# Five outer sums moved from VectorE to adding transfers, and two more pairs of products split into quarters

## The chip, the cores and the metric

The kernel runs on one core of a Trainium2 chip. The metric is the device time of one execution in microseconds (us). Engines are named as in the profile: PE is TensorE's matmul and PEld its weight load, DVE is VectorE, ACT is ScalarE, POOL is GpSimd, SP is SyncE, which issues most loads.

## What is computed

Eight batches of 256 tokens with 1024 features, in float32. Two layers, each with a residual:

```python
# layer 0, with a mask of its own for every batch b
sign = 2 * mask - 1                                  # (8, 1024, 1024)
x = x + (x @ W0.T + b0) + (x @ sign) * coeff[b]
# layer 1, with an adapter of rank 16 picked for every batch
x = x + (x @ W1.T + b1) + 2.0 * (x @ A[slot]) @ B[slot]
```

## The kernel before, in words

All data is kept transposed (features on the 128 partitions, tokens along the free dimension), so that the result of one layer is the moving operand of the next. The weight of layer 0 is made on the chip for each batch: ScalarE turns a block of the mask into numbers (line 453), VectorE adds the dense weight (line 364, `add`). The residual is an identity added to the weight.

Large products are made by Strassen's scheme in Winograd's form: seven products of half size in the place of eight, with sums of blocks before and after. Each level has four sums for the left factor (s1 to s4), four for the right factor (t1 to t4), and reads that add the products into the output.

- *First layer.* `seven(b)` (line 677) makes one batch by seven products (`product`, matmuls at line 720, 128 columns each). Its sums of weights and tokens are VectorE's. Product X of s3 and t3 is read by `finish(1, 1, "X")` (line 732 to 734), and afterwards TensorE adds the product of a22 and t4 into the same bank X; so that last product waits for this read.
- *Second layer.* After four batches (a group) `second_layer(group, before)` (line 968) multiplies W1 with the group's four results y, seen as one matrix of 2 x 2 blocks. Here Winograd's scheme stands twice: the outer seven products are the runs 0 to 6, in the order A11, A12, S1, S2, S4, S3, A22; a run is made of seven inner products of 256 x 256 x 256, four matmuls of 256 columns each (line 1003). The third run is S1, the fourth S2.

An outer sum of y (`outer_t`, line 978) makes a run's right factor: two instructions of 128x1024 on VectorE. The outer sums of W1 are made once, in the first group: S1, S3 and S2 by `outer_w1_moved` (line 903), a scaled copy on ScalarE (line 912) followed by a transfer from SBUF to SBUF that adds the other operand to it (line 920, issued by GpSimd); S4 on VectorE. The first group also stores all leaves of W1 (line 835, GpSimd's queue), and the second loads them again (`left_again`, line 853).

Some inner products are split a third time. Class `Deep` (line 1014) makes one of 256 x 256 x 256 from seven matmuls of 128 columns (line 1058), which accumulate in a chain: ScalarE copies the first (line 1071), VectorE takes sums out of the chain after the sixth and the seventh (lines 1080 and 1087). Each needs four sums of its left leaf and three instructions for its right factor (lines 1028 to 1037) first. `THIRD` names the runs whose products X (a11) and Z (s1) are made so, `LATE` those where Y (a12) and the last product into X (a22) are. Two methods of `Run` belong to it: `xz`, which issues the pair of quartered products and puts pieces of the run before (`rest`: its z4 and x4, or x3) between them, and `y4`, the same for the late pair, with pieces of x2 between. In a late run the first product is read directly into two outputs, where another run copies bank X to Y on ScalarE.

```python
THIRD = {1: (0, 2, 3, 4, 6)}
LATE = {1: (0, 1)}
BIG, SMALL, BANKS = 34, 16, 8
```

Buffers are 34 big ones (128x1024), 16 small ones (128x512) and the 8 banks of PSUM.

*The order of work.* Nothing is issued in the order of the code. Each instruction is a task of `Plan` with an engine, a duration, the tasks that it needs, and often a due time. TensorE's order is the program's; `order` (line 137) lays out the other engines by a simulation: for each engine the task that can start first, among equals the one with the earliest latest start, `ls`, worked back from when its readers are due. `ahead` bars a task until so long before that. The laid-out order is then fixed; on the chip each engine works through its own list and waits by semaphores. A transfer is taken to need its issue, a latency (2.8 us on POOL's queue) and its bytes at 396e3 per us. A task with `hop` set is one that TensorE waits for soon: VectorE is not given another task that would end over 0.05 us after such a task can start, or after its `ls` where that is later; if nothing shorter is there, VectorE is left idle.

Of the kernel before, what the change touches and what calls it, by code (L numbers as in the profile page):

```python
# [17 lines left out]
DENSE = (0,)  # L18
EARLY = (1,)
SCALING = 2.0  # L20
THIRD = {1: (0, 2, 3, 4, 6)}
LATE = {1: (0, 1)}
BIG, SMALL, BANKS = 34, 16, 8


# [29 lines left out]
class Plan:  # L55
# [10 lines left out]
    MARGIN = 0.3  # L66
    TIGHT = 1.0
    FAR = 3.0
    HOP = 0.05

    def __init__(self, start):
        self.tasks = []
# [3 lines left out]
    def task(self, engine, busy, tail, emit, reads=(), writes=(), due=None, ahead=None, nbytes=0):  # L76
        k = Task()
        k.engine, k.busy, k.tail, k.emit, k.due, k.ahead = engine, busy, tail, emit, due, ahead
        k.n, k.bytes, k.rank, k.hop = len(self.tasks), nbytes, None, False
# [12 lines left out]
        for r in writes:  # L92
            for key in r.keys:
                self.writer[r.buf, key] = k
                self.readers[r.buf, key] = []
        k.bufs = list(dict.fromkeys(r.buf for r in [*writes, *reads]))
        for b in k.bufs:
            b.left += 1
        k.open = len(k.before)
        k.ready = 0.0  # L100
        k.done = False
        if engine == "PE":
            k.due = self.pe
            self.pe += busy
        self.tasks.append(k)
        return k
# [30 lines left out]
    def order(self, slots, idle):  # L137
# [40 lines left out]
            return min(ok)  # L178

        out = []  # L180
        hops = [k for k in self.tasks if k.hop]
        while len(out) < len(self.tasks):
            best = None
            held = None
# [2 lines left out]
            for e in free:  # L187
# [8 lines left out]
                else:  # L196
# [15 lines left out]
                    elif soon and idle[e] and k.ls > s + self.FAR:  # L212
# [73 lines left out]
def kernel(  # L286
# [55 lines left out]
    def small(name, a, b):  # L342
        return Buf(name, "S", (a, b))
# [333 lines left out]
    def seven(b, leave=False):  # L677
# [143 lines left out]
    SOON = 12.0  # L821
    A_OF = {"a11": (0, 0), "a12": (0, 1), "a22": (1, 1)}

    def left_first(name):
        leaves = {n: w1_block(name, *uv) for n, uv in A_OF.items()}
        a = {(u, v): w1_block(name, u, v) for u in range(2) for v in range(2)}
        own = OWN.get(name, INNER)

        def keep(n):
            at = leaf_dram[name, n] = Buf(  # L830
                f"leaf_{name}_{n}",
                None,
                t=dram.tile([P, CG, OQ], F32, tag=f"{name}{n}", name=f"leaf_{name}_{n}"),
            )
            dma("POOL", at((0,)), leaves[n], P * 512 * 4, due=plan.pe + 25.0)

        for n in A_OF:
            if n in own:
                keep(n)
        for n, op, x, z in (  # L840
            ("s1", "add", a[1, 0], a[1, 1]),
            ("s2", "sub", "s1", a[0, 0]),
            ("s3", "sub", a[0, 0], a[1, 0]),
            ("s4", "sub", a[0, 1], "s2"),
        ):
            s = small(f"{name}_{n}", CG, OQ)
# [3 lines left out]
            keep(n)  # L850
        return leaves

    def left_again(name, pairs=()):
# [44 lines left out]
    def outer_w1(name, op, x, z, into=None):  # L898
        q = quads[name] = quads[into] if into else [pair(f"w1_{name}_{u}") for u in range(2)]
        for u in range(2):  # L900
            add(q[u](ALL), quads[x][u](ALL), quads[z][u](ALL), 1024, op)

    def outer_w1_moved(name, sign, x, z, into=None):

        q = quads[name] = quads[into] if into else [pair(f"w1_{name}_{u}") for u in range(2)]
        for u in range(2):
            o, a, b = (r(ALL) for r in (q[u], quads[x][u], quads[z][u]))
            plan.task(
                "ACT",
                1024 / 1200 + 0.06,  # L910
                0.11,
                lambda o=o, a=a: nc.scalar.mul(o.ap(), a.ap(), sign),
                (a,),
                (o,),
            )
            plan.task(
                "POOL",
                0.53,
                2.8,
                lambda o=o, b=b: nc.gpsimd.dma_start(o.ap(), b.ap(), accum_op=ALU.add),  # L920
                (o, b),
                (o,),
                nbytes=3 * P * 1024 * 4,
            )

    def behind(o, late):
        plan.task(
# [35 lines left out]
            )  # L963

    READ = (15.0, 4.0)
    UV = [(0, 0), (0, 1), (1, 1), (1, 0)]

    def second_layer(group, before):
# [45 lines left out]
        class Deep:  # L1014
# [62 lines left out]
            def second(self):  # L1077
                i = self.i
                u = self.chain((0,), lambda t: t[:, 0])
                k = add(self.quarter(0, 1), u, self.fifth.sb((i,), lambda t: t[:, i, 1]), P)  # L1080
                k.hop = True

            def third(self):
                i = self.i
                u = self.chain((0,), lambda t: t[:, :1].to_broadcast([P, 2, P]))
                o = self.ps((0,), lambda t: t[:, 1].rearrange("p (v o) -> p v o", v=2))
                k = add(o, u, self.fifth.sb(("zero", i), lambda t: t[:, i]), 2 * P)
                k.hop = True

        class Fifth:  # L1090

# [96 lines left out]
            return [("a11", "s1")] * (n in deep) + [("a12", "a22")] * (n in late)  # L1188

        def leaves_of(name):  # L1190
            left[name] = left_first(name) if first else left_again(name, pairs(OUTER.index(name)))

        class Run:
            def __init__(self, n, seed, out, dest=None, then=None):
# [383 lines left out]
```

## Time and profile before

| | |
|---|---|
| median of 3 runs | 398.2 us (397.63 to 399.25) |
| profiled execution, own time | 397.7 us |
| its span, first to last instruction | 396.0 us |
| clock granted to TensorE | 1.00 |
| PE busy | 392.3 us (99%), 2836 records |
| PEld busy | 363.2 us (92%) |
| DVE busy | 350.2 us (88%), 516 instructions |
| ACT busy | 154.2 us (39%), 281 instructions |
| POOL busy | 52.7 us (13%), 101 instructions |
| HBM, read and written | 64.25 and 19.92 MB |

One matmul in float32 shows as two records. In the span the dense first batch goes up to 34.8 us, the first layer of the first group to 109.8, its second layer to 202.5, the second group's first layer to 299 and its second layer to the end. Rows of the profile name the line of `kernel.py` that issued an instruction; most of VectorE's are line 364, so the shapes tell them apart. Durations of one instruction on VectorE are a little longer than the distance to the next, because neighbours overlap.

### The profile page before, as it was taken

How to read it: one execution, taken by the hardware profiler on the slowest of the kernel's cores; microseconds unless marked ns; L12 is line 12 of the kernel's file. 1: busy time of each engine (PE TensorE's matmuls, PEld its weight loads, DVE VectorE, ACT ScalarE, POOL GpSimd, SP SyncE). 2: the span in 40 equal slices, each digit the busy share in tenths (PEclk: the TensorE clock that was granted, in tenths of full speed). 3: DMA queues.
4: the chain of work that ended last, by engine and by line, in shares of the span. 5: the costliest groups of instructions: out<-in, count | busy, mean ns of one | idle time of the engine just before them, and what ended most of it. 6: DMA issues, size and time to landing. Idle time of an engine off the chain costs nothing.

```text
span 396.0 us, 7306 instructions
## 1 busy us (share of the span) xinstructions
PE 392.3 (99%) x2836; PEld 363.2 (92%) x2836; DVE 350.2 (88%) x516; ACT 154.2 (39%) x281; POOL 52.7 (13%) x101
## 2 busy tenths in 40 slices
PE   9999999999999999999999999999999999999997
PEld 7889999999978888888899999999999789998896
DVE  3559999999997789997999999999976989899876
ACT  5784675612534121008417276372222322210210
POOL 1000000131653353140134000000000000000000
PEclk9999999999999999999999999999999999999999
DMA  8999999460699889878479655111000357753844
GB/s 285 391 389 410 407 408 365 149 226 26 183 263 282 281 278 370 339 270 318 165 283 323 214 211 223 69 55 55 0 28 18 119 161 236 227 148 118 273 134 168
DMA packets 32724, 87.79 MB, mean 222 GB/s; under 512 B 4530, under 2 KB 5170, under 8 KB 32690
## 3 DMA queue, kind: packets, MB, share of 16 engines
q1 hardware_dynamic: 26064, 67.19, 47.5%
q0 software_dynamic: 6336, 19.94, 15.8%
q8 instruction: 22, 0.36, 0.4%
q10 hardware_dynamic: 290, 0.20, 0.2%
q14 instruction: 12, 0.10, 0.1%
HBM read 64.25 MB, written 19.92 MB: 213 GB/s over the span
## 4 chain that ended last, share of the span: by engine, by line
PE 99%; DVE 0%; issue 0%
PE bank L720 44%; PE bank L1003 37%; PE bank L534 7%; PE bank L1058 6%; PE bank L1162 2%; PE bank L1131 2%; PE bank L399 1%; PE bank L1352 0%; PE bank L412 0%; DVE big L364 0%
## 5 line engine op out<-in xcount | busy, mean ns | idle before, releaser
L364 DVE TENSOR_TENSOR big<-big,big 128x1024 f32<-128x1024 f32 (+2 forms) x112 | 115.0, 1044 | 3.2 <-PE bank L720 2.1
L720 PE MATMUL bank<-small,big 128*128 128x128 f32 x896 | 104.0, 275 | 0.0
L720 PEld LDWEIGHTS bank<-small,big 128*128 128x128 f32 x896 | 102.0, 192 | 0.0
L364 DVE TENSOR_TENSOR big<-bank,big 128x512 f32<-128x512 f32 (+2 forms) x107 | 70.6, 676 | 18.2 <-PE bank L1003 11.8
L720 PE MATMUL bank<-big,big 128*128 128x128 f32 x672 | 78.3, 275 | 0.0
L1003 PE MATMUL bank<-small,small 128*128 128x256 f32 x328 | 78.2, 380 | 0.0
L720 PEld LDWEIGHTS bank<-big,big 128*128 128x128 f32 x672 | 76.8, 192 | 0.1
L453 ACT ACTIVATE big<-big,neg_c,two_c 128x1024 f32<-128x1024 int32 (+2 forms) x65 | 70.6, 1124 | 9.9 <-DMA big<-mask 9.8
L364 DVE TENSOR_TENSOR big<-big,w 128x1024 f32<-128x1024 f32 (+2 forms) x65 | 67.7, 1073 | 6.0 <-ACT big L453 4.3
L1003 PEld LDWEIGHTS bank<-small,small 128*128 128x128 f32 x328 | 61.2, 190 | 8.6 <-issue 0.8
L631 ACT ACTIVATE big<-bank,b 128x128 f32<-128x128 f32 x112 | 32.0, 369 | 61.8 <-PE bank L720 61.8
L368 ACT COPY bank<-bank 128x512 f32<-128x512 f32 (+1 forms) x32 | 13.7, 430 | 91.7 <-PE bank L1058 35.4
L1003 PE MATMUL bank<-big,small 128*128 128x256 f32 x168 | 41.2, 380 | 0.0
L368 ACT COPY big<-bank 128x512 f32<-128x512 f32 x32 | 17.6, 593 | 53.2 <-PE bank L1162 27.4
L1003 PEld LDWEIGHTS bank<-big,small 128*128 128x128 f32 x168 | 30.8, 190 | 4.3 <-DVE big L364 0.4
L534 PE MATMUL bank<-small,big 128*128 128x256 f32 x128 | 29.3, 393 | 0.0
L534 PEld LDWEIGHTS bank<-small,big 128*128 128x128 f32 x128 | 25.3, 199 | 3.7
L364 DVE TENSOR_TENSOR small<-big,small 128x512 f32<-128x512 f32 (+1 forms) x49 | 27.5, 571 | 0.4
L1003 PE MATMUL bank<-big,big 128*128 128x256 f32 x112 | 26.7, 381 | 0.0
L1003 PEld LDWEIGHTS bank<-big,big 128*128 128x128 f32 x112 | 21.0, 190 | 3.4 <-DVE big L364 0.4
L1097 POOL MEMSET small<- 128x256 f32 x7 | 2.2, 310 | 155.1 <-PE bank L720 78.9
L1058 PE MATMUL bank<-small,big 128*128 128x128 f32 x154 | 22.4, 275 | 0.0
(59 smaller groups left out, 268.7 us busy)
## 6 DMA issues: line engine op xcount, KB each, us to landing
big<-mask SPq DMA_DIRECT2D x56, 512.0 KB, 7.3
big<-xT SPq DMA_DIRECT2D x14, 512.0 KB, 6.7
big<-mask SPq DMA_DIRECT2D x16, 256.0 KB, 5.4
w<-w0T SPq DMA_DIRECT2D x16, 256.0 KB, 5.4
big<-w1T SPq DMA_DIRECT2D x8, 512.0 KB, 5.8
leaf_S_s<-small POOLq DMA_DIRECT2D x16, 256.0 KB, 5.8
outT<-big POOLq DMA_DIRECT2D x16, 256.0 KB, 3.0
outT<-big SPq DMA_DIRECT2D x15, 256.0 KB, 2.3
```

The costliest lines, as they stand in the source:

```text
L364: return dve(lambda: f(o.ap(), x.ap(), y.ap()), n, (x, y), (o,), due, ahead)
L368: "ACT", n / 1200 + 0.06, 0.11, lambda: nc.scalar.copy(o.ap(), x.ap()), (x,), (o,), due
L399: nc.tensor.matmul(idle_ps.t[:, 0, :n], lhsT=zeros[:, :P], rhs=zeros[:, :n], start=True, stop=True)
L453: lambda: nc.scalar.activation(o.ap(), x.ap(), AF.Identity, bias=neg_c.t[:, b : b + 1], scale=two_c.t[:, b : b + 1]),
L534: nc.tensor.matmul(dense[ot // 2].t[:, ot % 2, :], lhsT=w_b0[c].t[:, h, j * P : (j + 1) * P], rhs=x0[c // CG].t[:, c % CG, :], start=c == ...
L631: lambda o=o, p=p, bias=bias: nc.scalar.activation(o.ap(), p.ap(), AF.Identity, bias=bias.ap()),
L720: nc.tensor.matmul(ps[:, j, :], lhsT=l[:, c, j * P : (j + 1) * P], rhs=m[:, 2 * a + c, :], start=first and a == 0 and c == 0 and j == 0, s ...
L1003: nc.tensor.matmul(ps.t[:, j, :], lhsT=lt[:, c, j * P : (j + 1) * P], rhs=rt[:, c, :], start=start and c == 0 and j == 0, stop=False, skip ...
L1058: lambda: nc.tensor.matmul(o.ap(), lhsT=l.ap(), rhs=r.ap(), start=start, stop=False, skip_group_check=True),
L1097: plan.task("POOL", 0.4, 0.1, lambda: nc.gpsimd.memset(z.ap(), 0.0), (), (z,), ahead=5.0)
L1131: nc.tensor.matmul(ph.t[i * S : i * S + R, 0, :], lhsT=la.t[:, i, c, :], rhs=y[GB * group + i, c // TPH].t[:, c % TPH, :], start=c == 0, s ...
L1162: nc.tensor.matmul(ps[b].t[:, j, :], lhsT=lb_pad.t[rows, o : o + P], rhs=h_sb.t[rows, :], start=j == 0, stop=j == 1, skip_group_check=True,)
```

## The change

The outer sums of y for S2 and A22 in the first group and for S2, S3 and A22 in the second are made as the moved sums of W1: a copy on ScalarE that turns the sign, and an adding transfer issued by GpSimd. A22 is now built in the buffers of S2 and no longer in those of a block of y. The first group's third run (S1) gets its products X and Z in quarters, for which `left_first` makes the sums of the leaves; with that, z4 of its second run is no longer issued at that run's end but between the quarters, and so is x4. The second group's fourth run (S2) gets the late pair too. The planner's figures for a moved sum change (0.9 us of issue for 0.53, two times the bytes for three). `hop` becomes a number, and the read of X at row 1, column 1 of each batch of the first layer gets one: -1.0, so that VectorE is kept free from 1 us before that read can start or has to start at the latest, whichever is later.

```diff
-THIRD = {1: (0, 2, 3, 4, 6)}
-LATE = {1: (0, 1)}
+THIRD = {0: (2,), 1: (0, 2, 3, 4, 6)}
+HOP, READ_HOP = 0.05, -1.0
+LATE = {1: (0, 1, 3)}
...
-                    if e == "DVE" and not k.hop and pe_at < len(pe):
+                    if e == "DVE" and k.hop is None and pe_at < len(pe):
                         lag = max(0.0, free["PE"] - pe[pe_at].due)
                         for h in [h for h in hops[:4] if not h.done]:
                             u = self.near(h, lag)
-                            if u is None or s >= u or s + k.busy <= max(u, h.ls) + self.HOP:
+                            if u is None or s >= u or s + k.busy <= max(u, h.ls) + h.hop:
                                 continue
-                            until = max(u, h.ls) + self.HOP
+                            until = max(u, h.ls) + h.hop
...
         def finish(i, v, n):
             o = y[b, i]((v,), lambda t: t[:, :, v * H : (v + 1) * H])
-            add(o, banks[n]((0,)), o, OH, due=plan.pe + 20.0)
+            k = add(o, banks[n]((0,)), o, OH, due=plan.pe + 20.0)
+            if n == "X" and i == 1 and v == 1:
+                k.hop = READ_HOP
...
-    def left_first(name):
+    def left_first(name, pairs=()):
...
+        leaves["deep"] = {}
+        for n in [n for two in pairs for n in two]:
+            l = leaves[n]
+            sums = small(f"ls_{name}_{n}", 4, P)
+            s = leaves["deep"][n] = [sums((i,), lambda t, i=i: t[:, i]) for i in range(4)]
...
+            for o, op, x, z in (
+                (s[0], "add", block(0, 1), block(1, 1)),
+                (s[1], "sub", s[0], block(0, 0)),
+                (s[2], "sub", block(0, 0), block(0, 1)),
+                (s[3], "sub", block(1, 0), s[1]),
+            ):
+                add(o, x, z, P, op, ahead=SOON)
         return leaves
...
+    def moved(o, sign, x, z):
+
+        plan.task(
+            "ACT", 1024 / 1200 + 0.06, 0.11, lambda: nc.scalar.mul(o.ap(), x.ap(), sign), (x,), (o,)
+        )
+        plan.task(
+            "POOL",
+            0.9,
+            2.8,
+            lambda: nc.gpsimd.dma_start(o.ap(), z.ap(), accum_op=ALU.add),
+            (o, z),
+            (o,),
+            nbytes=2 * P * 1024 * 4,
+        )
...
+    MOVED = (("S2", "A22"), ("S2", "S3", "A22"))
...
             for v in range(2):
-                add(whole(right[name][v]), whole(x[v]), whole(z[v]), 1024, "sub")
+                if name in MOVED[group]:
+                    moved(whole(right[name][v]), -1.0, whole(z[v]), whole(x[v]))
+                else:
+                    add(whole(right[name][v]), whole(x[v]), whole(z[v]), 1024, "sub")
...
-            outer_t("A22", b21, right["S2"], into=b21)
+            outer_t("A22", b21, right["S2"], into=right["S2"])
```

More of the change, by code (lines that the diff above doesn't have):

```diff
@@ L68 @@
     FAR = 3.0
-    HOP = 0.05
     def __init__(self, start):
@@ L78, in task @@
         k.engine, k.busy, k.tail, k.emit, k.due, k.ahead = engine, busy, tail, emit, due, ahead
-        k.n, k.bytes, k.rank, k.hop = len(self.tasks), nbytes, None, False
+        k.n, k.bytes, k.rank, k.hop = len(self.tasks), nbytes, None, None
         k.before, k.after = {}, []
@@ L180, in order @@
         out = []
-        hops = [k for k in self.tasks if k.hop]
+        hops = [k for k in self.tasks if k.hop is not None]
         while len(out) < len(self.tasks):
@@ L850, in left_first, with block @@
             keep(n)
+        leaves["deep"] = {}
[3 more added lines that the diff above has]
+            s = leaves["deep"][n] = [sums((i,), lambda t, i=i: t[:, i]) for i in range(4)]
+            def block(c, j):
+                return l.buf(l.keys, lambda t, f=l.index: f(t)[:, c, j * P : (j + 1) * P])
+            for o, op, x, z in (
[5 more added lines that the diff above has]
+                add(o, x, z, P, op, ahead=SOON)
         return leaves
@@ L906, in outer_w1_moved @@
         for u in range(2):
[L907 to L924, printed above, removed]
+            moved(q[u](ALL), sign, quads[x][u](ALL), quads[z][u](ALL))
     def behind(o, late):
@@ L1080, in second @@
                 k = add(self.quarter(0, 1), u, self.fifth.sb((i,), lambda t: t[:, i, 1]), P)
-                k.hop = True
+                k.hop = HOP
             def third(self):
@@ L1087, in third @@
                 k = add(o, u, self.fifth.sb(("zero", i), lambda t: t[:, i]), 2 * P)
-                k.hop = True
+                k.hop = HOP
         class Fifth:
@@ L1190, in leaves_of @@
         def leaves_of(name):
-            left[name] = left_first(name) if first else left_again(name, pairs(OUTER.index(name)))
+            left[name] = left_first(name, pairs(OUTER.index(name))) if first else left_again(name, pairs(OUTER.index(name)))
         class Run:
```

## The prediction

> **What bounds the kernel now.** I read the page first, then the chain of waits in order of time, the table by stage, and last the rows of the instructions that the change adds or removes. The page:
>
> ```profile
> span 396.0 us, 7306 instructions
> PE 392.3 (99%) x2836; PEld 363.2 (92%) x2836; DVE 350.2 (88%) x516; ACT 154.2 (39%) x281; POOL 52.7 (13%) x101
> ...
> PE   9999999999999999999999999999999999999997
> ...
> PE 99%; DVE 0%; issue 0%
> ```
>
> TensorE is busy for 392.3 of 396.0 us, and the chain that ended last is TensorE for 99%. A busy digit alone does not prove a dense stream, since ends are modelled; so the chain in order of time, which goes by starts (start, length, what):
>
> ```profile
> 327.08 2.23 PE bank L1058 x20
> ...
> 358.08 9.07 PE bank L1003 x42
> ...
> 391.41 1.77 PE bank L1352 x12
> 393.18 0.02 issue
> 393.20 0.29 DVE big L364
> ```
>
> A matmul of this program shows as two records. 9.07/42 = 0.216 us per record of 256 columns and 2.23/20 = 0.1115 us per record of 128 columns; every long piece of the chain has these two pitches, so TensorE stands still almost nowhere. What isn't its work is 396.0 - 392.3 = 3.7 us, and nearly all of that is the start (first matmul at 0.9 us) and the end (last one done at 393.2), which the change doesn't touch. So the kernel's time is the count of its matmuls. Other engines only matter where they make TensorE wait. By stage (first layer, second layer, for each of the two groups; columns: length, busy time of PE, PEld, DVE, ACT, POOL, clock, DMA share, GB/s):
>
> ```profile
> 34.80:109.80 75.00, 75.00 (x674) 75.00 (x673) 74.53 (x87) 37.61 (x73) 13.88 (x24) 1.00 0.71 261
> 109.80:202.50 92.70, 92.70 (x523) 79.00 (x522) 80.99 (x114) 27.57 (x42) 30.03 (x53) 1.00 0.86 288
> 202.50:299.00 96.50, 96.50 (x867) 96.50 (x866) 91.79 (x108) 45.19 (x87) 5.91 (x12) 1.00 0.38 135
> 299.00:396.00 97.00, 94.16 (x641) 83.48 (x639) 83.59 (x170) 20.19 (x50) 1.56 (x5) 1.00 0.51 163
> ```
>
> VectorE is nearly full in the first layers, and has 11.7 and 13.4 us free in the second layers, where the change works. The transfers' share is 0.86 in the first group's second layer and 0.51 in the second group's.
>
> One rule of the Trainium skill reads this otherwise: "Perfetto Trace Analysis", section "Identifying the Most-Contended Engine", says that matmul busy time is no measure of the headroom and that weight-load busy time is. By it 396.0 - 363.2 = 32.8 us would be open; the chain's pitches leave 3.7 us, and I go by them.
>
> **TensorE's work (the gain).** A product of 256 x 256 x 256 is four matmuls of 256 columns: 8 records x 0.216 = 1.73 us. As quarters it is seven of 128 columns: 14 x 0.1115 = 1.56 us. That saves 0.167 us each; 0.16 with the pitch of 0.112 that longer runs of 128 columns show (34.81 to 109.85 us, 672 records). Four products change: X and Z of the first group's third run, and Y and the last product into X (the leaves a12 and a22) of the second group's fourth. 4 x 0.16 = 0.64 us, all on the path, because TensorE is the path. Nothing else in the diff removes a matmul. z4 and x4 of the first group's second run move into the gaps between the quarters, z4 and x3 of the second group's fourth into the next run's; their count stays.
>
> **VectorE.** Removed: ten outer sums of 128x1024, four in the first group (S2, A22) and six in the second (S2, S3, A22), at 1.22 us in the rows by form: 4.9 and 7.3 us. Added in the first group: 8 sums of 128 columns for the left quarters (0.28 each: 2.3), per product one of 256 and two of 128 for the right ones (0.42 + 0.57: 2.0 for both), and the two sums that feed TensorE's next quarter, which have rows of their own:
>
> ```profile
> L364 DVE TENSOR_TENSOR bank<-bank,small 128x256 f32<-128x256 f32 x14 | 5.4, 428 | 3.1 <-PE bank L1058 3.1
> L364 DVE TENSOR_TENSOR bank<-bank,small 128x128 f32<-128x128 f32 x14 | 3.5, 293 | 1.4 <-PE bank L1058 1.4
> ```
>
> 0.43 + 0.29, twice: 1.4. Together 5.7 against 4.9 removed: 0.8 us more in a stage with 11.7 us free. In the second group: four left sums of 256 columns (1.7), right ones 2.0, feeding ones 1.4, and two more reads of a bank, since a product is now read into two outputs (2 x 0.69 = 1.4): 6.5 against 7.3, 0.8 us less. So for VectorE the transfers pay for the quarters and neither leaves a gain; it wasn't the path. What hides these sums is the free time of the second layers. Were that cover gone, they would cost what doesn't fit, at most the 5.7 and 6.5 us.
>
> The new reservation (VectorE is kept free from 1 us before the read at line 734 of each batch's lower right product) adds no work but can hold VectorE idle in the first layers. Bounds: a gain is excluded, as no matmul of line 720 waits there now; the loss is up to 1.0 us plus one 1.22 us sum per batch, three batches of the first group where only 0.47 us is free: 3 x 2.2 - 0.5 = 6.1 us. I take 0: the read's turn comes while 16 other matmuls (3.6 us) stand before the product that needs it.
>
> **ScalarE, GpSimd, queues.** Ten scaled copies at 1.06 us (the row of line 912) go to ScalarE, which is busy 27.6 of 92.7 and 20.2 of 97.0 us. In return the fourth run's 0.57 us copy falls away; four copies of a quarter (0.25) and two of a pair (0.37) come. Queued behind a scaled copy are copies out of banks that TensorE reuses, so one may come 1.06 us later; the waits of ScalarE on TensorE (35.4 us on line 1058) say that it is early as a rule. GpSimd issues ten transfers:
>
> ```profile
> L920 POOL DMA_DIRECT2D big<-big x6: 876/900/1231, 104.8 to 131.5; - x6
> ...
> DMA to landing us min/median/max: 4.8/7.2/11.0
> ```
>
> That is 9 us of issue. GpSimd waits in order for the scaled copy before each, and behind it in the first group stand stores of leaves and of output, whose late landing holds buffers; in the second only the small memsets for the quarters (0.31 us). A moved sum now takes 1.06 + 0.9 + 7.2, some 9 us, where VectorE took 1.22. The trace says that there is time: VectorE does pairs of 128x1024 sums at 113.64 and 117.12 us, and the third run's inner sums for the next factor start only past 139 us.
>
> ```profile
> 113.64 2.35 DVE L364 TENSOR_TENSOR big<-big,big 128x1024 f32<-128x1024 f32 x2
> ...
> 139.19 1.28 DVE L364 TENSOR_TENSOR small<-big,small 128x512 f32<-128x512 f32 x2
> ```
>
> Even 11.0 us fits into 25. The second group has the same length of run and half-free transfers. So cost 0, with an upper bound below. The skill's "DMA: Bandwidth & Descriptors", section on the anatomy of a DMA on the gpsimd path, gives 2.0 us plus bytes/436e3, an estimate of 3.2 us for 512 KB; these rows show 7.2, and the rows decide.
>
> **New waits.** Quarters have a chain of their own: TensorE, ScalarE's copy, VectorE's sum, TensorE. The fourteen quartered products now in the trace (196 records of line 1058) lose almost nothing: the worst piece is 12 records in 1.47 us where 12 x 0.1115 = 1.34, 0.13 us in all. For two pairs more I take 0 and keep 0.3 us as the upper end.
>
> **Sum.** The profiled execution took 397.7 us, its span 396.0, so 1.7 lie around it. 397.7 - 0.64 = 397.06. The median of the runs is 398.2, 0.5 above the profiled one; on that footing the sum is 397.56, and I predict **397.6 us**.
>
> **Rivals.** (1) *The new quarters stall a little.* Each of four products has two feeding sums; at 0.08 us each, half of the shortest wait of VectorE on a quarter in its timeline (0.16 us), 8 x 0.08 = 0.64 us eats the gain: 398.2. For it: VectorE is busy 15.70 of the 16.6 us from 131.4 to 148, where the first group's pair falls, and its first quarter comes a product (1.73 us) sooner than the third run starts now. Against it: 196 records of quarters with 0.13 us lost.
>
> (2) *A moved sum lands late and holds VectorE, slower.* Place: the first group, where transfers are busiest (shares of 1.05 and 1.02 from 109.8 to 131.4 us and 1.00 from 148 to 164). VectorE's order is fixed beforehand with a landing of 0.9 + 2.8 + 1.05 MB / 396e3 = 6.35 us; if it is 11.0, the first inner sum stands at the head of VectorE's queue for up to 4.6 us, and behind it the reads and the feeding sums that TensorE waits for. TensorE never makes that up: 398.2 - 0.64 + 4.6 = 402.2, or about 400.4 for a wait of 2.8. It decides from where the wait outlasts what TensorE has in hand by 2.6 us. For it: 11.0 us stands in the rows, and six transfers of the same kind share the queue then. Against: the 25 us above.
>
> (3) *Faster by more than 2 us*: needs stalls to remove, and the 3.7 us are start and end. Only chance between runs is left.
>
> That the quarters or transfers aren't made as described can't be excluded but has no sign in the diff.
>
> **How the numbers follow.** Forecast 0.53, rival 1 0.15: both within 0.5% (2.0 us, about what a measurement of this kernel can tell from no change). Rival 2 0.20, and other waits of that size (the reservation's, late buffers) 0.07: slower, 0.27. Rival 3 0.05: faster. The runs of before spread from 397.63 to 399.25, -0.6 and +1.0 about their median; 397.6 with that and 0.3 of stall makes 397.0 to 398.9 for the forecast alone. The range must reach into rival 2: 396.7 to 401.2.
>
> **What would show it.** Right: line 1058 (or its new number) with 56 more records, the product line with 32 fewer, PE busy near 391.7, still no PE wait behind VectorE, and the last matmul done near 392.5. VectorE's busy time within 1 us of 350.2, ScalarE's up by 11. Wrong: pieces of the chain with a pitch above 0.112 or 0.216 us, or with VectorE or a transfer in them; where they lie (after 136 us, after 340 us, or in the first layers) would tell rivals 1, 2 and the reservation apart.

## The result, and the profile after

The changed kernel takes 401.12 us (399.97 to 401.95, six runs) against 397.76 us of the kernel before in the same runs: a ratio of 1.0076, interval 1.0054 to 1.0099. It is slower, where no change was forecast; it lies inside the stated range (396.7 to 401.2) because that range was stretched to reach into rival 2. The page of the profiled execution (401.16 us):

```profile
span 399.5 us, 7452 instructions
PE 392.9 (98%) x2860; PEld 363.6 (91%) x2860; DVE 348.1 (87%) x540; ACT 164.9 (41%) x296; POOL 62.4 (16%) x113
...
PE   9999999999999999979999999999999999999997
...
PEclk9999999999999999989999999999999999999999
...
PE 55%; DVE 20%; DMA 19%; issue 4%; POOL 1%; SPq 1%; POOLq 0%; DVEq 0%
```

PE has 24 records more, as 56 of the quarters less 32 of the split products make, yet it fills less of the span. One slice of its busy row is a 7, the clock's row has an 8 in the same slice, and the chain that ended last is TensorE's for only 55%, where it was 99%. The chain in order of time (start, length, what) shows what came in:

```profile
161.19 11.88 DMA big<-big
...
173.09 0.70 DVE small L364
...
175.71 0.61 DVE big L364
...
176.37 2.91 PE bank L1022 x8
```

It is read upwards from TensorE: its product at 176.37 waited for a read by VectorE (175.71), that stood behind an inner sum (173.09), and that one waited for an adding transfer, issued at 161.19 us and landed 11.88 us later. After 176.37 TensorE waits for nothing that long again. VectorE and TensorE at that place, and TensorE in the kernel before:

```profile
168.54 0.69 DVE L364 TENSOR_TENSOR big<-bank,big 128x512 f32<-128x512 f32 x1 [0.30 <-PE bank L1022]
173.09 0.69 DVE L364 TENSOR_TENSOR small<-big,big 128x512 f32<-128x512 f32 x1 [3.86 <-DMA big<-big]
```

```profile
171.72 1.89 PE L1022 MATMUL bank<-big,small 128*128 128x256 f32 x8
176.37 2.91 PE L1022 MATMUL bank<-small,big 128*128 128x256 f32 x8 [2.75 <-DVE big L364]
179.21 2.72 PE L1181 MATMUL bank<-h,lb 32*128 32x256 f32 x32
181.86 1.99 PE L1022 MATMUL bank<-big,big 128*128 128x256 f32 x8
```

```profile
172.62 1.89 PE L1003 MATMUL bank<-big,small 128*128 128x256 f32 x8
174.35 1.89 PE L1003 MATMUL bank<-small,big 128*128 128x256 f32 x8
176.17 2.01 PE L1162 MATMUL bank<-h,lb 32*128 32x256 f32 x32
178.11 1.99 PE L1003 MATMUL bank<-big,big 128*128 128x256 f32 x8
```

VectorE stood still for 3.86 us, and TensorE for 2.75. I go by starts, since ends are modelled. From the product ahead of the wait to the next it takes 4.65 us (171.72 to 176.37), 1.73 in the kernel before: the wait costs 2.92. The eight records after it then took 2.84 us (1.82 before) and the 32 short ones of line 1181 took 2.65 (1.94 before): the clock had gone down. In the table by stage, cut where the clock changes, it reads 0.50 for 3.41 us (columns as before: length, PE, PEld, DVE, ACT, POOL, clock, DMA share, GB/s):

```profile
176.37:177.30 0.93, 0.93 (x4) 0.85 (x5) 0.93 (x2) 0.00 (x0) 0.71 (x2) 1.00 1.03 418
177.30:180.71 3.41, 3.41 (x21) 2.30 (x24) 2.70 (x5) 0.00 (x0) 2.03 (x4) 0.50 0.97 376
180.71:184.00 3.29, 3.29 (x34) 2.66 (x27) 2.48 (x4) 2.16 (x5) 0.13 (x1) 1.00 0.93 283
```

That costs (2.84 - 1.82) + (2.65 - 1.94) = 1.73 us, half of the 3.41. The balance of the two profiled executions: before this place the changed one was ahead by 0.90 us (171.72, against 172.62). 0.54 of it was there when the first layer ended, and is chance: the dense first batch ended 0.83 us earlier (the last section says why), and 0.30 of that was lost near 105 us. The rest is the first pair of quarters, 0.32 by the count. Then 2.92 + 1.73 = 4.65 us are lost and 0.32 won by the second pair: -0.90 + 4.65 - 0.32 = 3.43 of the 3.5 us by which the spans differ.

The transfer is the second of the first group's A22. ScalarE's copies for it come when TensorE has read S2 for the last time, because A22 is built in the buffers of S2:

```profile
158.11 1.06 ACT L924 ACTIVATE big<-big 128x1024 f32<-128x1024 f32 x1 [2.87 <-PE bank L1022]
159.84 1.06 ACT L924 ACTIVATE big<-big 128x1024 f32<-128x1024 f32 x1 [0.67 <-PE bank L1022]
```

Between 158 us and VectorE's first sum for A22 there are 11 us, not the 25 of S2. The two transfers were issued at 159.67 and 161.19 us and landed after 10.9 and 11.9 us. The transfer engines had been full since the first layer's end:

```profile
131.40:148.00 16.60, 16.60 (x93) 14.91 (x92) 15.78 (x30) 3.19 (x7) 10.00 (x19) 1.00 1.00 328
148.00:160.00 12.00, 12.00 (x57) 10.58 (x56) 11.86 (x19) 2.38 (x4) 4.11 (x9) 1.00 1.01 369
```

The kernel before has a share of 0.81 in the first of these stretches and 1.00 in the second.

### The profile page after: what moved, and what is told of

Same layout as the page of the kernel before. It is cut to its first block, busy times and chain, and to the rows that moved or that the text cites. A ratio compares the mean times of both kernels' runs of the same rounds, so it can differ in the third digit from the quotient of the medians.

```text
span 399.5 us, 7452 instructions
## 1 busy us (share of the span) xinstructions
PE 392.9 (98%) x2860; PEld 363.6 (91%) x2860; DVE 348.1 (87%) x540; ACT 164.9 (41%) x296; POOL 62.4 (16%) x113
## 4 chain that ended last, share of the span: by engine, by line
PE 55%; DVE 20%; DMA 19%; issue 4%; POOL 1%; SPq 1%; POOLq 0%; DVEq 0%
PE bank L720 25%; PE bank L1022 21%; DVE big L364 13%; DMA big<-big 9%; PE bank L1077 6%; DMA big<-mask 4%; DMA w<-w0T 3%; DVE small L364 3%; DMA leaf_S_s<-small 2%; DVE big L609 2%; DVE small L705 2%; PE bank L1181 2%; PE bank L1150 1%; SPq L377 1%; POOL big L930 1%
## 5 line engine op out<-in xcount | busy, mean ns | idle before, releaser
L364 DVE TENSOR_TENSOR big<-big,big 128x1024 f32<-128x1024 f32 (+2 forms) x104 | 103.9, 1015 | 4.9 <-PE bank L720 3.3
L720 PE MATMUL bank<-small,big 128*128 128x128 f32 x896 | 104.1, 275 | 0.0
L720 PEld LDWEIGHTS bank<-small,big 128*128 128x128 f32 x896 | 102.0, 192 | 0.2 <-DVE big L364 0.2
L364 DVE TENSOR_TENSOR big<-bank,big 128x512 f32<-128x512 f32 (+2 forms) x109 | 71.8, 676 | 18.5 <-PE bank L1022 10.9
L720 PEld LDWEIGHTS bank<-big,big 128*128 128x128 f32 x672 | 76.8, 192 | 0.1
L1022 PE MATMUL bank<-small,small 128*128 128x256 f32 x312 | 74.8, 380 | 0.0
L1022 PEld LDWEIGHTS bank<-small,small 128*128 128x128 f32 x312 | 58.0, 190 | 8.1 <-issue 0.8
L368 ACT COPY bank<-bank 128x128 f32<-128x128 f32 (+1 forms) x35 | 13.9, 406 | 79.7 <-PE bank L1077 37.1
L1022 PEld LDWEIGHTS bank<-big,small 128*128 128x128 f32 x160 | 29.1, 190 | 4.0 <-DVE big L364 0.4
L930 POOL DMA_DIRECT2D big<-big x16 | 14.5, 928 | 106.5 <-DVE small L364 71.3
L534 PEld LDWEIGHTS bank<-small,big 128*128 128x128 f32 x128 | 24.6, 193 | 3.6 <-DVE big L364 0.2
L1077 PE MATMUL bank<-small,big 128*128 128x128 f32 x178 | 25.6, 275 | 0.0
L1022 PE MATMUL bank<-big,big 128*128 128x256 f32 x104 | 24.8, 381 | 0.0
L1077 PEld LDWEIGHTS bank<-small,big 128*128 128x128 f32 x178 | 23.8, 192 | 0.8
```

The lines of the kernel that those rows point to most:

```text
L364: return dve(lambda: f(o.ap(), x.ap(), y.ap()), n, (x, y), (o,), due, ahead)
L368: "ACT", n / 1200 + 0.06, 0.11, lambda: nc.scalar.copy(o.ap(), x.ap()), (x,), (o,), due
L534: nc.tensor.matmul(dense[ot // 2].t[:, ot % 2, :], lhsT=w_b0[c].t[:, h, j * P : (j + 1) * P], rhs=x0[c // CG].t[:, c % CG, :], start=c == ...
L720: nc.tensor.matmul(ps[:, j, :], lhsT=l[:, c, j * P : (j + 1) * P], rhs=m[:, 2 * a + c, :], start=first and a == 0 and c == 0 and j == 0, s ...
L930: lambda: nc.gpsimd.dma_start(o.ap(), z.ap(), accum_op=ALU.add),
L1022: nc.tensor.matmul(ps.t[:, j, :], lhsT=lt[:, c, j * P : (j + 1) * P], rhs=rt[:, c, :], start=start and c == 0 and j == 0, stop=False, skip ...
```

## The experiments

The theory from these views: the first group's A22 lands late, VectorE's fixed order has its inner sum ahead of reads that TensorE needs, and TensorE stops. Rival A: the new quarters need more of VectorE than it has. Rival B: the reservation for the first layer's read. Ratios are to the kernel before, run beside each.

**A22 summed by VectorE.**

```diff
-    MOVED = (("S2", "A22"), ("S2", "S3", "A22"))
+    MOVED = (("S2",), ("S2", "S3", "A22"))
```

> The changed kernel with the first group's A22 summed by VectorE again (two sums of 128x1024), in the buffers of S2; the other four sums stay moved. Theory (the first group's moved A22 lands late and holds VectorE): the one wait of TensorE of 2.75 us near 173 us and the lowered clock after it are gone; no VectorE wait on a transfer there; ratio to before 0.998 to 1.000, about 397.1 us (397.76 less 0.64). Rival A (the quarters of the first group need more of VectorE than it has, and the wait is where that shows): the wait stays, or moves by a few us, and the time stays near 400 us or above, since VectorE gets 2.4 us more work. Rival B (the reservation for the first layer's read does it): the time stays near 401 us.

Measured: 397.63 us, ratio 0.9994 (0.9983 to 1.0006). The wait is gone, TensorE goes from 171.92 to 175.46 without a gap. Rivals A and B fall as the cause of the 3 us. Not all of the 0.64 us is seen: the interval holds both 0.9984 and 1.000.

**A22 moved, and nothing else of the change.**

```diff
-                add(whole(right[name][v]), whole(x[v]), whole(z[v]), 1024, "sub")
+                if name == "A22" and first:
+                    moved(whole(right[name][v]), -1.0, whole(z[v]), whole(x[v]))
+                else:
+                    add(whole(right[name][v]), whole(x[v]), whole(z[v]), 1024, "sub")
...
-            outer_t("A22", b21, right["S2"], into=b21)
+            outer_t("A22", b21, right["S2"], into=right["S2"] if first else b21)
```

> The kernel before with one edit: the first group's A22 made by the scaled copy and the adding transfer, in the buffers of S2. No further quarters, no reservation, no other moved sum. Theory: the same late landing holds VectorE at A22's first inner sum, a TensorE wait of 1 to 4 us between 165 and 180 us; ratio 1.003 to 1.012 (399 to 402.5 us). The transfer may land a little earlier than in the changed kernel, since S2's two transfers aren't in the queue before it. Rivals A and B: nothing of theirs is in this kernel, so ratio 1.000.

Measured: 397.73 us, ratio 0.9995 (0.9985 to 1.0005): this missed. VectorE at the same sum:

```profile
170.82 0.69 DVE L364 TENSOR_TENSOR small<-big,big 128x512 f32<-128x512 f32 x1 [0.66 <-DMA big<-big]
```

It waits, but for 0.66 us only, and TensorE doesn't. The transfers, issued at 160.39 and 162.11 us, landed after 7.8 and 8.6 us. So A22 is necessary (the run above) and not enough: something else makes its landing 3 us later.

**The inner sums of A22 held back.**

```diff
-            add(t["t1"], rb(name, 0, 1), rb(name, 0, 0), 512, "sub")
+            add(t["t1"], rb(name, 0, 1), rb(name, 0, 0), 512, "sub", ahead=ahead)
...
-            add(t["t3"], rb(name, 1, 1), rb(name, 0, 1), 512, "sub")
+            add(t["t3"], rb(name, 1, 1), rb(name, 0, 1), 512, "sub", ahead=ahead)
...
-            inner_t("A22")
+            inner_t("A22", 6.0 if first else None)
```

> The changed kernel, with A22 moved as there, but two of the first group's inner sums for A22 (t1, t3, and so those that follow from them) may not be laid out earlier than 6 us before they are due. Theory (not the late landing itself costs time, but that a sum waiting for it stands at the head of VectorE's fixed order far ahead of its need): the transfers land as late as before, 10 to 12 us after their issue, and TensorE waits no more near 173 us; ratio 0.998 to 1.000. Rival (the transfer is late even for the run that needs it, at about 190 us): a wait of over 1 us remains. Rival A: a wait remains, ratio over 1.004.

Measured: 398.33 us, ratio 1.0012 (1.0000 to 1.0025). A22's transfers landed after 10.9 and 11.9 us, as late as in the changed kernel, and neither VectorE nor TensorE waited for them. So the lateness costs nothing by itself; the place of the first reader in VectorE's order does. The ratio still missed. The profiled execution, at 400.51 us the slowest of ten, has the same pattern elsewhere, in the second group, with a load of a leaf in the place of the adding transfer:

```profile
338.21 0.43 DVE L364 TENSOR_TENSOR big<-big 128x256 f32<-128x256 f32 x1 [2.63 <-DMA big<-leaf_S_s]
```

```profile
345.38 0.71 PE L1077 MATMUL bank<-small,big 128*128 128x128 f32 x4 [1.60 <-DVE bank L364]
```

The first sum of a late pair's leaves waits 2.63 us for its load, and the new quarters of the second group's fourth run, 7 us later, wait 1.60 us for VectorE's feeding sum. The same sum waited 0.65 us in the changed kernel's profile, without a wait of TensorE. Whether the other nine executions lost by it isn't shown.

**A22 in buffers of its own.**

```diff
-            outer_t("A22", b21, right["S2"], into=right["S2"])
+            outer_t("A22", b21, right["S2"], into=None if first else right["S2"])
```

> The changed kernel, with the first group's A22 in two buffers of its own and no longer in those of S2. Its scaled copy then need not wait until TensorE has read S2 for the last time (158 us in the changed kernel). Theory: the copies run some 10 us earlier, the transfers land before VectorE's first inner sum of A22 (169 us), no wait of TensorE there; ratio 0.998 to 1.000. If the queue of GpSimd is what makes it late whatever its start, the wait stays: ratio 1.004 to 1.010.

Measured: 397.77 us, ratio 0.9997 (0.9985 to 1.0008). A22's transfers are issued at 132.04 and 133.99 us and land at 142.8 and 145.5, 10.7 and 11.5 us later, long before their reader; no wait near 173 us. So their latency is as bad, and only the start in S2's buffers made it matter. A wait of 0.66 us at 343 us remains, as in the run before.

**Without the reservation.**

```diff
-                k.hop = READ_HOP
+                k.hop = None
```

> The changed kernel without the reservation for the first layer's read (its task has no hop value again). Theory (the first group's A22 lands late and holds VectorE): the TensorE wait of over 1 us between 170 and 180 us stays, ratio 1.004 to 1.010. Rival B (the reservation): the wait is gone, ratio near 0.999. Beside it the wait of 0.2 to 0.3 us at line 720 near 105 us, which the changed kernel has and the one before has not, should go if the reservation makes it.

Measured: 400.0 us, ratio 1.0055 (1.0037 to 1.0072). The wait stays, rival B falls. The reservation changes the place of two groups of rows in VectorE's order, near 80 and 224 us, and nothing else. The 0.3 us near 105 us are gone and 0.4 us near 81 us came, but neither can be laid to the reservation: the order near 105 us is the same, and waits near 80 and 106 us stand in one profile of a kernel with the reservation and not in another of the very same kernel (the two runs with S2 summed, below). What is different is what follows the wait:

```profile
176.43 1.99 PE L1022 MATMUL bank<-small,big 128*128 128x256 f32 x8 [2.14 <-DVE big L364]
```

After a wait of 2.14 us the eight records take 1.92 us from start to start and the 32 short ones 2.16, not the 2.84 and 2.65 of the changed kernel: no stretch at half the clock. (This trace holds no clock record, so its 1.00 in the views says nothing.)

**The quarters without the transfers.**

```diff
-    MOVED = (("S2", "A22"), ("S2", "S3", "A22"))
+    MOVED = ((), ())
```

> The changed kernel with none of the five sums moved: both new pairs of quarters and the reservation stay. VectorE has 5.7 us more work in the first group's second layer (of 11.7 free) and 6.5 in the second's (of 13.4 free). Theory as the prediction had it (VectorE has room): TensorE's work falls by 0.64 us and little is lost, ratio 0.998 to 1.001. Rival A (VectorE has no room for the quarters without the transfers): waits of TensorE behind VectorE in the second layers, over 1 us together, ratio over 1.002.

Measured: 399.19 us, ratio 1.0039 (1.0023 to 1.0055). Rival A has a share, but not where it was looked for: there is no wait over 0.1 us between 110 and 200 us. TensorE ends at 393.8 us, 0.6 later than before in spite of less work: 0.34 of it was there when the first layer began, and its longest wait in the second group is 0.25 us, at 390. VectorE then works on its last reads without a break past the end of TensorE:

```profile
387.06 2.35 DVE L364 TENSOR_TENSOR big<-big,big 128x1024 f32<-128x1024 f32 x2
...
391.12 3.25 DVE L364 TENSOR_TENSOR big<-bank,big 128x512 f32<-128x512 f32 x7
```

The kernel before ends these reads at 393.5, this one at 394.4 us. That makes 4.1 us from TensorE's last start to the end, where the kernel before and the changed one take 3.1.

**A longer landing in the plan.**

```diff
             "POOL",
             0.9,
-            2.8,
+            8.4,
             lambda: nc.gpsimd.dma_start(o.ap(), z.ap(), accum_op=ALU.add),
```

> The changed kernel with one figure changed: the planner takes an adding transfer to land 8.4 us after its issue and not 2.8, plus its bytes (so 11.95 us in all; the changed kernel's landed after 11.9). Theory (the order was laid out for a landing of 6.35 us): VectorE's inner sums of A22 stand later in its order, behind reads that TensorE needs, and TensorE does not wait there: ratio 0.998 to 1.001, with transfers that land as late as before. If not the estimate but the transfer's lateness for the run itself costs time: ratio over 1.004.

Measured: 400.02 us, ratio 1.0049 (1.0032 to 1.0066). The wait near 173 us is gone; A22's transfers were issued at 162.93 and 164.25 us and landed after 6.5 and 7.7. But the figure holds for W1's moved sums as well, and the order laid out anew has two waits of TensorE of 1.2 us at 140 and 143 us, in the new quarters, behind a VectorE that waits for adding transfers (2.00 us at 137 and 1.54 at 142). So the expected time was missed: one figure for all adding transfers, whose landings differ from 5 to 15 us, puts some reader in a wrong place.

**S2 summed by VectorE, A22 moved.**

```diff
-    MOVED = (("S2", "A22"), ("S2", "S3", "A22"))
+    MOVED = (("A22",), ("S2", "S3", "A22"))
```

> The changed kernel with the first group's S2 summed by VectorE again and its A22 moved. With A22 moved alone in the kernel before, the transfers landed 7.8 and 8.6 us after their issue and cost nothing. If S2's two transfers are what fills GpSimd's queue: A22's land after 8 to 9 us here too, the wait shrinks to under 0.5 us, ratio 0.998 to 1.001. If it is the quarters (other work shifted, more small sums): A22's land after 11 to 12 us and the wait of 2 to 3 us stays, ratio 1.004 to 1.010.

Measured: 397.53 us, ratio 0.9989 (0.9980 to 0.9999). A22's transfers, issued at 159.83 and 161.38 us as in the changed kernel, land after 6.4 and 7.3 us. The same kernel once more:

> The changed kernel with the first group's S2 on VectorE and its A22 moved, the same as the run above at 0.9989, with more rounds. Theory (0.64 us less work for TensorE, most of it kept): ratio 0.9980 to 0.9995 with an interval that leaves out 1.000.

397.84 us, ratio 0.9999 (0.9989 to 1.0009). This missed. The wait is gone (the slowest of the 22 executions took 398.83 us, the changed kernel's fastest 399.97), but whether this version gains is not settled.

**S2 and A22 moved, without the quarters.**

```diff
-                add(whole(right[name][v]), whole(x[v]), whole(z[v]), 1024, "sub")
+                if name in ("S2", "A22") and first:
+                    moved(whole(right[name][v]), -1.0, whole(z[v]), whole(x[v]))
+                else:
+                    add(whole(right[name][v]), whole(x[v]), whole(z[v]), 1024, "sub")
```

(with A22 in S2's buffers, as in the run with A22 alone)

> The kernel before with the first group's S2 and A22 both moved, and nothing else of the change (no further quarters, no reservation, nothing moved in the second group). A22 moved alone cost nothing there; A22 moved beside a summed S2 in the changed kernel cost nothing either. Theory (the two S2 transfers fill the transfer engines' queue from 115 us on, and what is issued at 160 us still lands 10 us later): A22's transfers land 10 to 12 us after their issue, TensorE waits 1 to 3 us near 173 us, ratio 1.003 to 1.008. If the quarters' shifted work is needed for it: landing after 8 to 9 us, no wait, ratio 1.000.

Measured: 402.7 us, ratio 1.0132 (1.0110 to 1.0155).

```profile
174.37 0.69 DVE L364 TENSOR_TENSOR small<-big,big 128x512 f32<-128x512 f32 x1 [3.66 <-DMA big<-big]
```

```profile
177.65 3.68 PE L1021 MATMUL bank<-small,big 128*128 128x256 f32 x8 [3.16 <-DVE big L364]
```

The pattern is complete without one new quarter. In one point it was not as expected: the transfers landed 6.9 and 8.0 us after their issue, but were issued 4.3 to 4.5 us later than with A22 alone (164.92 and 166.37 us). GpSimd works in order, and ahead of them stood stores of leaves that waited in their turn.

**Nothing moved in the first group.**

```diff
-    MOVED = (("S2", "A22"), ("S2", "S3", "A22"))
+    MOVED = ((), ("S2", "S3", "A22"))
```

> The changed kernel with none of the first group's sums moved, the second group's three as there. Both pairs of quarters and the reservation stay. With only A22 moved in the first group the time was 0.9989 of before. Theory (VectorE has room for the first group's quarters, the transfers there bring nothing): ratio 0.998 to 0.9995, no TensorE wait over 0.5 us between 110 and 200 us, and the first group's leaf stores land some 2 to 4 us sooner than in the changed kernel. Rival A (VectorE needs the transfers there too): waits of over 0.5 us in that stretch, ratio over 1.000.

Measured: 397.35 us, ratio 0.9990 (0.9981 to 0.9999), the lowest median of all and a little below both kernels; PE is busy 391.6 us, and no TensorE wait over 0.1 us stands between 110 and 200 us. VectorE does have the room there: its busy time is 352.5 us. The gain is no more settled than that of the version with S2 summed, whose first interval also left out 1.000.

**The second group's part alone.**

```diff
-THIRD = {0: (2,), 1: (0, 2, 3, 4, 6)}
+THIRD = {1: (0, 2, 3, 4, 6)}
...
-    MOVED = (("S2", "A22"), ("S2", "S3", "A22"))
+    MOVED = ((), ("S2", "S3", "A22"))
```

> The changed kernel without the first group's quarters and without its moved sums: left are the second group's late pair, its three moved sums and the reservation. By the count of matmuls TensorE has 0.32 us less work than before (two products): ratio 0.999 if nothing is lost, with the busy time of TensorE's rows down by 0.3 us; 1.000 to 1.002 if the new quarters near 342 us wait for their leaves, as they did for 0.7 and 1.6 us in two of the runs above.

Measured: 398.18 us, ratio 1.0012 (1.0003 to 1.0021): no gain, though it has 0.32 us less work. The profiled execution shows small waits of 0.1 to 0.4 us near 46, 80, 106, 281 and 331 us, in the first layers mostly, whose order the edit doesn't aim at. The first three lost about what an early start had won: the first layer began at 33.56 us, where it began at 34.65 in the kernel before, and ended at 109.77, against 109.69. Why this order keeps less than the one above isn't settled.

**Queue or load.** Two edits to the changed kernel: the stores of S2's and S4's leaves from another engine's queue, and the second group's masks later.

```diff
-            dma("POOL", at((0,)), leaves[n], P * 512 * 4, due=plan.pe + 25.0)
+            dma("ACT" if name in ("S2", "S4") else "POOL", at((0,)), leaves[n], P * 512 * 4, due=plan.pe + 25.0)
```

> The changed kernel, with the 14 stores of the leaves of S2 and S4 issued by ScalarE and not by GpSimd. The bytes are the same. Queue theory: A22's transfers no longer stand behind them, land 4 to 7 us after their issue (11 and 12 in the changed kernel), and TensorE waits under 0.5 us near 173 us: ratio 0.998 to 1.001. Load theory (the engines are full, whichever queue the bytes come from): they land after 9 us or more and the wait of over 1.5 us stays: ratio 1.003 to 1.009.

Measured: 400.17 us, ratio 1.0064 (1.0041 to 1.0087). In the profiled execution A22's transfers landed after 5.9 and 7.8 us with the engines as full as ever (1.01 from 148 to 174 us), and no one waited for them, as the queue theory expects. The time did not follow: ScalarE now stood in line with the stores (issues that lasted 5.5 us for two) and VectorE behind it, and TensorE waited 0.9 us at 161:

```profile
159.23 1.23 DVE L364 TENSOR_TENSOR big<-big,big 128x1024 f32<-128x1024 f32 x1 [3.29 <-ACT big L368]
```

That execution is the fastest of eight (398.74 us); what the slower ones wait for isn't shown.

```diff
-        dma("SP", m, mask[b, i * NG + g], P * CG * OH * 4, ahead=AHEAD)
+        dma("SP", m, mask[b, i * NG + g], P * CG * OH * 4, ahead=AHEAD if b < GB else 6.0)
```

> The changed kernel, with the loads of the second group's masks barred until 6 us before they are due, where it was 18. The order of buffers changes with it, so waits may come elsewhere, in the second group's first layer above all. Load theory: the transfer engines' share from 131 to 160 us falls clearly below 1.00, A22's transfers land 4 to 7 us after their issue and no TensorE wait of over 1 us is left near 173 us. Queue theory: they still land after 9 us or more, and the wait stays.

Measured: 402.08 us (two runs), ratio 1.0115 (1.0042 to 1.0188). The share stayed at 1.01 in both stretches from 131 to 160 us, A22's transfers landed after 11.0 and 11.8 us and the wait stayed (2.64 us). The load was not taken down, so this edit says nothing of it.

The traces say more than the two edits do. A share of 1.0 tells that the engines are busy, not how much is waiting for them. That can be counted: the transfers that were issued and had not landed (as far as the trace tells landings) when the first of A22's two was issued. Stores are 256 KB, loads 512 KB; the stores come from GpSimd, in one run some from ScalarE, and the loads from SyncE.

| run | stores and loads not landed | landing of A22's first |
|---|---|---|
| stores by ScalarE | 2 and 2: 1.5 MB | 5.9 us |
| S2 summed, A22 moved | 3 and 2: 1.75 MB | 6.4 us |
| S2 and A22 without the quarters | 7 and 1: 2.25 MB | 6.9 us |
| A22 alone | 5 and 2: 2.25 MB | 7.8 us |
| the changed kernel | 6 and 4: 3.5 MB | 10.9 us |
| masks later | 6 and 4: 3.5 MB | 11.0 us |

The landing goes with all the bytes that are outstanding, not with GpSimd's alone: by these the third row would be the latest. So the stores issued by ScalarE don't speak for the queue either; in that run less than half of the load was outstanding. With S2 moved and A22 summed (the first experiment) the same 6 and 4 are outstanding at 160 us, with neither moved 3 and 2. The runs with the sums held back and without the reservation (6 and 4; 10.9 and 10.4 us) and with the longer landing in the plan (3 and 2; 6.5 us) fit too. Bytes aren't the whole measure, though: at 132 us, in the run with A22 in buffers of its own, 2.25 MB with two adding transfers among them went with 10.7 us; in the changed kernel the engines moved 249 GB/s at a share of 1.05 from 109.8 to 131.4 us, and 369 at 1.01 from 148 to 160.

**What the runs make together.** In the first group, moved sums and their cost:

| | without the new quarters | with them |
|---|---|---|
| neither S2 nor A22 | 1.000 (before) | 0.9990 |
| S2 alone | not tried | 0.9994 |
| A22 alone | 0.9995 | 0.9989, 0.9999 |
| both | 1.0132 | 1.0076 |

Either sum can be moved for nothing; both together cost 3 to 5 us, with the quarters or without. S2's two transfers come at 114 to 115 us to engines that are full until 160; what GpSimd issues afterwards starts or lands 3 to 5 us later (W1's next adding transfer, at 122.4 us, lands after 13.2 us, and after 8.6 with S2 summed), and A22, which can't begin before 158 us, is read 11 us after. The table of bytes speaks for the load of the shared engines as what carries the delay; no edit changed that load alone.

## Why the prediction was wrong

*TensorE's work* was right: 56 records more of line 1077, 32 fewer of line 1022, and PE busy for 391.6 us in two versions without the wait (391.7 was expected). VectorE's busy time fell by 2.1 us, where within 1 was expected, and that cost nothing. The new quarters of the first group lose nothing there. Those of the second do in some executions, 0.7 and 1.6 us, by a late leaf, for which the 0.3 us kept as the upper end were too little; rival 1 had the size, not the cause.

*The moved sums at cost 0* is the step that failed. "Even 11.0 us fits into 25" was worked out from the rows of S2 at 113 and 139 us, and then used for all five. A22's own times were left out: the code puts it into S2's buffers, so it starts after S2's last product, and the distance to its reader is 11 us. By the prediction's own figures, 1.06 + 0.9 + 11.0 is 13 us, 2 more than there were. Also, 11.0 us was taken as the worst landing, from a trace without the transfers that the change adds to a stage with a share of up to 1.05; they landed after up to 15.0 us.

*Rival 2* named the mechanism, the first group, the order of VectorE and a wait of up to 4.6 us; VectorE's was 3.86. Its price of 402.2, or 400.4 for a wait of 2.8, encloses the 401.12, in part by luck: it set VectorE's wait equal to TensorE's loss, and those were 3.86 and 4.65 us. Its chance of 0.20 was too low, for the reason above: the evidence put against it belonged to another sum. "Half-free transfers" held the second group to be safe: no read waited for an adding transfer there in the changed kernel's profile, only for a leaf.

*The price of a wait* lacked a term: after 2.75 us of idling TensorE ran at half the clock for 3.41 us, 1.7 us more.

*VectorE* was held to have room in both second layers, so that the transfers bring nothing. For the first group that is right (0.9990 with none moved there). For the second it is wrong: with none moved there either the ratio is 1.0039. The 13.4 us free were a mean over the stage, and the end, where VectorE's last reads set the time (1.0 us more there), has none to spare. *The reservation* at 0 was right within what these runs can tell.

## What to carry to other kernels

A cost of nothing must be shown for each instance of an edit: read when its inputs are free, when it is first read, and compare that with a landing in the queue as the change will fill it. In an engine with a fixed order the price of a late operand is set by what stands behind its first reader, so hold that reader back or start the transfer sooner before giving up the transfer. Two edits that are free one by one may load the same transfer engines: run them together and singly, and count what is outstanding, since a share of 1.0 doesn't tell.

## What the runs showed of the hardware that was not expected

*A wait of TensorE can cost more than its length.* After waits of 2.64 us (masks later), 2.75 (the changed kernel) and 3.16 (both sums moved) the granted clock was 0.50 for 3.41 us, with records of 256 columns 0.427 us apart, about twice their 0.216:

```profile
177.69:181.10 3.41, 3.41 (x8) 2.46 (x8) 2.30 (x4) 0.00 (x0) 2.30 (x5) 0.50 1.01 351
```

After 2.14 us the records kept their pitch. What decides between 2.14 and 2.64 isn't shown. Nor is it the same in every execution: one such stretch makes a mean clock of 0.996, and of the changed kernel's six runs four have 0.995 or 0.996, while the fastest (399.97 us) has 1.000, as a run without clock records would show too. The Trainium skill, "TensorE: Matmul & The Clock Gate", section "What's actually happening", ties the lower clock to an idle window of some 3.4 us that runs freely; here waits of 2.64 and 2.75 us were enough, and the measurement decides.

*Every execution begins slowly, and not for the same time.* The first records of 256 columns come 0.427 us apart too:

```profile
3.17 2.50 PE L399 MATMUL bank<-const-float32-0.0 128*128 128x256 f32 x6
```

This lasts until 8.5 us in the kernel before's profile and 6.6 in the changed kernel's, and moves the start of the first layer: from 33.55 to 35.26 us over the profiled executions. In two executions of one kernel (S2 summed, A22 moved) it began at 33.55 and 34.30 us; the earlier one then took 75.80 us for the first layer, with small waits near 80 and 106 us, and the later one 75.04, with none. So a difference of up to a microsecond between two profiled executions can be chance, and the prediction, which took 0.216 us for the pitch of every long piece of the chain, passed over these first microseconds.
